# A written-out issue order for batches 2 to 30 of a cross-attention kernel, which gives VectorE's long subtraction another place beside GpSimd's operations

## The chip, the cores and the metric

The kernel runs on one core of a Trainium2 chip. The metric is the device time of one execution in microseconds (us). Five engines of the core take their instructions each from a queue of its own and in order: TensorE (matrix products; PE in the profile, its weight loads PEld), VectorE (DVE), ScalarE (ACT), GpSimd (POOL) and SyncE (SP), which here only issues DMAs. An instruction that waits on a semaphore holds back everything behind it in its queue.

## The reference

For each of 32 batches there are 512 query rows of x with 640 columns, and 77 context rows with 1024 columns. Queries come from x, keys and values from the context; 20 heads of 32 columns; softmax over the 77 keys; the heads' outputs go through an output matrix, and bias and x are added. The reference also names three more groups of keys, which are empty here because there are only 77 context rows. All data are float32.

```
q = heads(x @ to_q_w); k = heads(ctx @ to_k_w); v = heads(ctx @ to_v_w)
p = softmax(q k^T / sqrt(32))
out = merge(p v) @ to_out_w + to_out_b + x
```

## The kernel before

**Precision.** Every float32 matrix product is done as three products of a high and a low part. The high part is a rounded copy (ScalarE), the low part is the rest, value minus high part (VectorE or GpSimd).

**Stages.** A first stage of about 250 us projects the context into keys and values, which go to scratch in DRAM. Then come 160 slots, n = 0 to 159: five slots j = 0 to 4 for each batch b, n = 5b + j. Slot n does heads 4j to 4j+3 of its batch, and because the work is a pipeline, it does parts of several slots at once:

- queries of slot n+1: 15 matmuls (L443, `queries`), their split in `split_q`: high part on ScalarE (L454), two copies on GpSimd (L458), two low parts on VectorE (L460);
- scores of slot n, four tiles of 128 queries (L478, `scores`), each followed by a row maximum on VectorE (L486) and by four exponentials on ScalarE (L496, `exps`);
- softmax of slot n-1: reciprocal of the sums on VectorE (L506, `sums`), normalisation on GpSimd (L511, `normalize`), transposition on VectorE (L518, `transpose_p`), four stores to DRAM (L525);
- the probabilities of slot n-3 are loaded back from DRAM (L534 and L535, `load_p`), for use one slot later;
- those of slot n-4 are split: high parts on ScalarE (L542 and L543, `cast_p`), the small low part on GpSimd (L556, `last_p`), the large low part on VectorE (L549, `rest_p`, 128 x 1024: this is the long low-part subtraction). Then come six matmuls with the values (L570, `values`), and their two halves are added (L581 on ScalarE, L583 twice on VectorE, `sum_a`);
- the attention output of slot n-5 is split (L590 on ScalarE, `high_a`; L595 on VectorE, `low_a`). L595 reads the same PSUM tile that the six value matmuls of slot n-4 then write, and there is one such tile, so these matmuls wait for L595;
- eight steps of three matmuls of the output projection of an earlier batch (L613, `project`, in the order of `STEPS`), closed by VectorE's addition of bias and residual (L642) and by a store.

For the next batch, x is loaded (L253), transposed on VectorE (L257) and split (L264 on ScalarE, L265 on GpSimd). GpSimd also adds the bias to the residual (L606) and copies halves of the keys (L423, L424).

**Order.** The tile framework's scheduling is off (`manual_schedule`): each engine runs its instructions in the order in which the program issues them, and the framework only places the semaphores. `slot(n)` writes this order, the same for every batch from the third on. On VectorE, for one slot, it is: maximum 0, reciprocal, maximum 1, the long subtraction (L549), L595, maximum 2, two query low parts, maximum 3, transposition, then two halves of `sum_a` (in slots j = 4, L595 stands ahead of maximum 1). On GpSimd it is: last_p, normalize, two query copies, then bias or x work. Since `rs = sums(n - 1)`, `last_p` and `normalize` stand together in the program, and `rest_p` behind the second score tile:

```
s = scores(n, 0)
...
rs = sums(n - 1) if n else None
...
    last_p(taken)
...
    normalize(n - 1, rs)
exps(n, 0, *s)
...
s = scores(n, 1)
if taken is not None:
    rest_p(taken)
```

Of the kernel before, what the change touches and what calls it, by code (L numbers as in the profile page):

```python
# [8 lines left out]
F32 = mybir.dt.float32  # L9
FPR = mybir.dt.float32r  # L10
AF = mybir.ActivationFunctionType
ALU = mybir.AluOpType
# [39 lines left out]
def kernel(  # L52
# [202 lines left out]
    def transpose_x(b, i):  # L255
        part = xss[b][:, 4 * i : 4 * i + 4, :].rearrange("p a u -> p (a u)")
        nc.vector.transpose(part, part)  # L257

    def split_x(b, c, high=nc.scalar.copy, low=nc.gpsimd):

        xt = xpool[0].tile([P, 2, S], FPR, tag="xt", name="xt", bufs=7)
        src = xss[b].rearrange("p (a t) u -> p t a u", t=NQ)[:, :, :, c * Q : (c + 1) * Q]
        parts = [xt[:, i, :].rearrange("p (t a j) -> p t a j", t=NQ, j=Q) for i in range(2)]
        high(parts[0], src)  # L264
        low.tensor_tensor(parts[1], src, parts[0].bitcast(F32), ALU.subtract)  # L265
        xts[b, c] = xt

    ctx.enter_context(tc.manual_schedule(engines=ENGINES))

# [120 lines left out]
    psv = tc.alloc_tile_pool(name="psv", bufs=3, space=PSUM, side="right", reuse_waits="tile")  # L390
    late = []

    raws, pps, ats, pds, sms, pqs, pas, xrs, pos = ({} for _ in range(9))

    bias = main.tile([P, C], F32, name="bias")
    kbs, vbs, pnb = [], [], []
# [11 lines left out]
        vb = main.tile([P, nj, 2, 2, P], FPR, name=f"vb{g}")  # L408
        vbs.append(vb)

    def load_keys(b, g, heads=range(HPC)):
        j0, nj = GROUPS[g]
        src = k_dram[g][:, :, :, b * NKEY : (b + 1) * NKEY].bitcast(F32)
        kb = kbs[g].bitcast(F32)
        for i in heads:
            own, half = slice(i * HD, (i + 1) * HD), slice(i % 2 * NKEY, (i % 2 + 1) * NKEY)
            other = slice(*((i + 2) % HPC * HD + k for k in (0, HD)))
            for part, rows in enumerate((own, other)):
                nc.sync.dma_start(kb[rows, 1 + i // 2, :, half], src[own, part])

    def copy_keys(g):
        kb = kbs[g]
        nc.gpsimd.tensor_copy(kb[:64, 0], kb[:64, 1].bitcast(F32))  # L423
        nc.gpsimd.tensor_copy(kb[64:, 3], kb[64:, 2].bitcast(F32))  # L424

    def load_values(b, g, segments=SEGMENTS):
        j0, nj = GROUPS[g]
# [9 lines left out]
    def queries(n, k0, k1):  # L437
        b, j = divmod(n, NC_)
        if k0 == 0:
            pqs[n] = ps.tile([P, S], F32, tag="pq", name="pq", bufs=1)  # L440
        for k in range(k0, k1):
            for m, (a, c) in enumerate(PAIRS):
                nc.tensor.matmul(  # L443
                    pqs[n],
                    wq_s[:, k, a, j * P : (j + 1) * P],
                    xts[b, k][:, c, :],
                    start=(k == 0 and m == 0),
                    stop=(k == NC_ - 1 and m == 2),
                )
# [11 lines left out]
                qt[r, 1 + w, :], pq[r], qt[r, 0, :].bitcast(F32), ALU.subtract  # L461
            )

    def scores(n, t):
        b, j = divmod(n, NC_)
        g = GROUP_OF[j]
        qt, kb = qts[n % 2], kbs[g]
        jg = j - GROUPS[g][0]
        sc = ps.tile([P, S], F32, tag="sc", name="sc", bufs=3)
        half = KCOLS // 2  # L470
        for m, (cols, keys_) in enumerate(
            (
                (slice(0, KCOLS), kb[:, 0::3, jg]),
                (slice(0, half), kb[:, 1, jg]),
                (slice(half, KCOLS), kb[:, 2, jg]),
            )
        ):
            nc.tensor.matmul(  # L478
                sc[:, cols],
                qt[:, m, t * P : (t + 1) * P],  # L480
                keys_,
                start=(m == 0),
                stop=(m == 2),
            )
        nm = main.tile([P, HPC], F32, tag="nm", name="nm", bufs=3)
        nc.vector.tensor_reduce(  # L486
            nm, sc[:, :KCOLS].rearrange("p (h k) -> p h k", k=NKEY), AX.X, ALU.max, negate=True
        )
        return sc, nm

    def exps(n, t, sc, nm):
        if t == 0:
            sms[n] = main.tile([P, NQ * HPC], F32, tag="sm", name="sm", bufs=2)
        for i in range(HPC):
            at = t * HPC + i
            nc.scalar.activation(  # L496
                pnb[n % 2][:, at, :NKEY],
                sc[:, i * NKEY : (i + 1) * NKEY],
                AF.Exp,
                bias=nm[:, i : i + 1],  # L500
                accum_out=sms[n][:, at : at + 1],
            )

    def sums(n):
        rs = main.tile([P, NQ * HPC], F32, tag="rs", name="rs", bufs=2)
        nc.vector.reciprocal(rs, sms.pop(n))  # L506
        return rs

    def normalize(n, rs):
        pf = pnb[n % 2][:, :, :NKEY]  # L510
        nc.gpsimd.tensor_tensor(  # L511
            pf, pf, rs.unsqueeze(2).to_broadcast([P, NQ * HPC, NKEY]), ALU.mult
        )

    def transpose_p(n):
# [6 lines left out]
        pd = dram.tile([(NBLK + 2) * Q, S], F32, tag="pd", name="pd", bufs=6)  # L522
        rows = pd[: NBLK * Q].rearrange("(b i) q -> i b q", i=Q)
        for a in range(4):
            nc.sync.dma_start(  # L525
                rows[:, :, a * P : (a + 1) * P],
                z[a * Q : (a + 1) * Q].rearrange("p b t j -> p b (t j)"),
            )
        pds[n] = pd

    def load_p(n):
        pd = pds.pop(n)
        raw = late[0].tile([P, 3, S], F32, tag="raw", name="raw", bufs=2)
        nc.sync.dma_start(raw[:, 0:2, :], pd.rearrange("(k p) q -> p k q", k=2)[:P])  # L534
        nc.sync.dma_start(raw[:64, 2, :], pd[P : P + 64, :])  # L535
        raws[n] = raw

    def cast_p(n):

        raw = raws[n]  # L540
        pp = late[0].tile([P, 5, S], FPR, tag="pp", name="pp", bufs=1)
        nc.scalar.copy(pp[:64, 4, :], raw[:64, 2, :])  # L542
        nc.scalar.copy(pp[:, 0:2, :], raw[:, 0:2, :])  # L543
        pps[n] = pp

    def rest_p(n):

        raw, pp = raws.pop(n), pps[n]
        nc.vector.tensor_tensor(  # L549
            pp[:, 2:4, :], raw[:, 0:2, :], pp[:, 0:2, :].bitcast(F32), ALU.subtract  # L550
        )

    def last_p(n):

        raw, pp = raws[n], pps[n]
        nc.gpsimd.tensor_tensor(  # L556
            pp[64:, 4, :], raw[:64, 2, :], pp[:64, 4, :].bitcast(F32), ALU.subtract
        )
# [2 lines left out]

    PASSES = [(p, t, c + p * (t == 0)) for t, c in ((0, 0), (1, 4), (0, 2)) for p in range(2)]

    def values(n):
        b, j = divmod(n, NC_)
        g = GROUP_OF[j]
        pp, vb = pps.pop(n), vbs[g][:, j - GROUPS[g][0]]
        pas[n] = late[1].tile([P, 2, S], F32, tag="pa", name="pa", bufs=1)
        for p, t, c in PASSES:
            nc.tensor.matmul(  # L570
                pas[n][:, p, :],
                vb[:, p, t, :],
                pp[:, c, :],
                start=(c == p),
                stop=(c == p + 2),
            )

    def sum_a(n):
        pa = pas[n]
        aw = late[0].tile([64, 2, S], F32, tag="aw", name="aw", bufs=1)  # L580
        nc.scalar.copy(aw, pa[64:])  # L581
        for p in range(2):
            nc.vector.tensor_tensor(pa[64 * p : 64 * p + 64, 0], pa[:64, p], aw[:, p], ALU.add)  # L583

    def high_a(n):
        if n >= N - NC_ + 1:
            at = xpool[0].tile([P, 2, S], FPR, tag="xt", name="at", bufs=7)
        else:
            at = late[0].tile([P, 2, S], FPR, tag="at", name="at", bufs=8)
        nc.scalar.copy(at[:, 0, :], pas[n][:, 0])  # L590
        ats[n] = at

    def low_a(n):
        at = ats[n]
        nc.vector.tensor_tensor(  # L595
            at[:, 1, :], pas.pop(n)[:, 0], at[:, 0, :].bitcast(F32), ALU.subtract
        )

    def load_residual(b, t, xr=None):
# [28 lines left out]
    def piece(b, i):  # L628
        for t, h, j in STEPS[CUTS[i] : CUTS[i + 1]]:
# [3 lines left out]
            if j == NC_ - 1:  # L633
                closed.append((b, t, h))

    def finish():

        while closed:
            b, t, h = closed.pop(0)
            xr = xrs[b, t]  # L640
            cols = slice(h * HALF, (h + 1) * HALF)
            nc.vector.tensor_tensor(  # L642
                xr[:, cols], pos.pop((b, t, h))[:, :HALF], xr[:, cols], ALU.add
            )
            if (b, t) == (B - 1, NQ - 1):
                nc.sync.dma_start(out[b, t * P : (t + 1) * P, cols], xr[:, cols])
            elif h == 1:
                nc.sync.dma_start(out[b, t * P : (t + 1) * P, :], xr)

    LATE = 3  # L650
    LAG = 4
# [36 lines left out]
    def slot(n, beside=()):  # L688
# [135 lines left out]
        for i in turns[2]:  # L824
            transpose_x(b + 1, i)

    def end():


# [146 lines left out]
```

## Time and profile before

| | |
|---|---|
| three runs | 1928.79, 1928.88 and 1929.89 us, median 1928.88 us |
| profiled execution | span of 1928.2 us from its first to its last instruction; its time outside the span is not listed apart |
| TensorE matmul | 1882.9 us busy |
| VectorE, ScalarE, GpSimd | 1619.6, 1527.4 and 1423.9 us busy |
| HBM | 222 GB/s over the span |

The span is one execution; the runs are others, and their median lies 0.7 us above that span. Busy times are sums over stages that differ: the first 250 us have little softmax in them, and the last slots drain the pipeline. Between 354.3 and 1770.2 us the program repeats the same batch 28 times; the tables of the prediction are taken from there.

### The profile page before, as it was taken

What the parts mean: (1) busy time and instruction counts of PE and PEld (TensorE: products, weight loads), DVE (VectorE), ACT (ScalarE), POOL (GpSimd) and SP (SyncE); (2) the same over time, 40 slices, a digit from 0 to 9 for tenths busy, and PEclk for the clock granted to TensorE, in tenths of its full rate; (3) what the DMA queues carried; (4) which work ended last, traced back from release to release, by engine and by line L of the source; (5) the groups of instructions that cost most, each with busy time, mean ns of one, the idle gap of its engine ahead of it and who ended that gap; (6) DMA issues with size and microseconds to landing.
All of it is one profiled execution on the core that took longest, in us unless ns stands there. A gap on an engine that the chain in (4) does not pass through costs nothing.

```text
span 1928.2 us, 37543 instructions
## 1 busy us (share of the span) xinstructions
PE 1882.9 (98%) x10332; PEld 1663.1 (86%) x10332; DVE 1619.6 (84%) x2494; ACT 1527.4 (79%) x6210; POOL 1423.9 (74%) x1116
## 2 busy tenths in 40 slices
PE   9999997999999999999999999999999999999997
PEld 7888896898888888888888888988888888888887
DVE  4444447899999999999999999999999899999885
ACT  3232248998889898898898889998999889989883
POOL 1100067888888888888888888888888888888874
PEclk9999998999999999999999999999999999999999
DMA  9978868989999899888998998988889989988875
GB/s 185 205 194 248 198 180 218 229 232 234 233 225 235 231 232 225 229 234 231 233 231 228 228 238 236 237 231 232 237 232 227 228 223 232 227 231 229 225 202 166
DMA packets 565022, 431.36 MB, mean 224 GB/s; under 512 B 191120, under 2 KB 473168, under 8 KB 564816
## 3 DMA queue, kind: packets, MB, share of 16 engines
q1 hardware_dynamic: 559760, 413.62, 84.9%
q0 software_dynamic: 4416, 14.34, 2.2%
q8 instruction: 85, 1.39, 0.3%
q14 instruction: 121, 0.99, 0.2%
q10 hardware_dynamic: 640, 1.02, 0.2%
HBM read 247.17 MB, written 181.64 MB: 222 GB/s over the span
## 4 chain that ended last, share of the span: by engine, by line
PE 38%; DMA 22%; ACT 14%; DVE 9%; SPq 7%; POOL 5%; issue 5%; ACTq 0%; DVEq 0%; POOLq 0%
PE po L613 10%; PE pq L443 9%; DMA raw<-pd 8%; DMA xs<-in_x_dram 7%; ACT pn L496 6%; PE pv L191 5%; PE pk L191 5%; PE pa L570 4%; PE sc L478 4%; DVE pp L549 3%; DMA kb<-k_dram 2%; ACT pp L543 2%; SPq L432 2%; ACT pp L542 1%; ACT xt L264 1%
## 5 line engine op out<-in xcount | busy, mean ns | idle before, releaser
L496 ACT ACTIVATE pn<-sc,nm 128x77 f32<-128x77 f32 x2560 | 793.8, 332 | 46.6 <-DVE nm L486 40.6
L613 PE MATMUL po<-wo_s,at 128*128 128x320 f32 x3840 | 635.1, 314 | 12.1 <-DVE at L595 9.0
L443 PE MATMUL pq<-xt,wq_s 128*128 128x512 f32 x2400 | 623.7, 401 | 0.0
L613 PEld LDWEIGHTS po<-wo_s,at 128*128 128x128 f32 x3840 | 568.3, 189 | 20.4 <-DVE at L595 17.4
L496 ACT ACTIVATION_READ_ACCUMULATOR pn<-sc,nm 128x1 f32 x2560 | 544.6, 213 | 0.0
L511 POOL TENSOR_TENSOR pn<-pn,rs 128x1232 f32<-128x1232 f32 x160 | 507.7, 3173 | 33.3 <-DVE rs L506 24.2
L443 PEld LDWEIGHTS pq<-xt,wq_s 128*128 128x128 f32 x2400 | 431.3, 190 | 76.1
L478 PEld LDWEIGHTS sc<-kb,qt 128*128 128x128 f32 x1920 | 327.8, 189 | 57.2 <-POOL qt L458 8.7
L478 PE MATMUL sc<-kb,qt 128*128 128x154 f32 (+1 forms) x1920 | 318.1, 274 | 11.0 <-POOL qt L458 4.5
L486 DVE TENSOR_REDUCE nm<-sc 128x4 f32<-128x308 f32 x640 | 287.7, 450 | 37.7 <-PE sc L478 33.2
L549 DVE TENSOR_TENSOR pp<-raw,pp 128x1024 fp32r<-128x1024 f32 x160 | 253.1, 1582 | 40.7 <-ACT pp L543 38.7
L556 POOL TENSOR_TENSOR pp<-raw,pp 64x512 fp32r<-64x512 f32 x160 | 209.3, 1308 | 100.2 <-ACT pp L542 90.5
L570 PE MATMUL pa<-pp,vb 128*128 128x512 f32 x960 | 263.7, 404 | 15.3 <-DVE at L595 10.1
L518 DVE STREAM_TRANSPOSE z<-pn 128x1280 f32<-128x1280 f32 x160 | 241.8, 1511 | 9.3 <-DMA pd<-z 2.7
L460 DVE TENSOR_TENSOR qt<-pq,qt 64x512 fp32r<-64x512 f32 x320 | 219.1, 685 | 29.0 <-ACT qt L454 22.7
L583 DVE TENSOR_TENSOR pa<-pa,aw 64x512 f32<-64x512 f32 x320 | 222.6, 696 | 24.3 <-ACT aw L581 14.0
L265 POOL TENSOR_TENSOR xt<-xs,xt 128x512 fp32r<-128x512 f32 x160 | 202.6, 1291 | 37.1 <-ACT xt L264 32.5
L570 PEld LDWEIGHTS pa<-pp,vb 128*128 128x128 f32 x960 | 169.7, 188 | 63.4 <-DVE pp L549 15.4
L606 POOL TENSOR_TENSOR xr<-xr,bias 128x640 f32<-128x640 f32 x128 | 202.7, 1585 | 17.3 <-DMA xr<-in_x_dram 5.4
L458 POOL CAST qt<-qt 64x512 fp32r<-64x512 f32 x320 | 194.8, 609 | 23.7 <-ACT qt L454 4.2
L581 ACT COPY aw<-pa 64x1024 f32<-64x1024 f32 x160 | 161.9, 1012 | 48.2 <-PE pa L570 44.1
L542 ACT CAST pp<-raw 64x512 fp32r<-64x512 f32 x160 | 99.5, 622 | 99.7 <-DMA raw<-pd 95.6
(46 smaller groups left out, 1640.9 us busy)
## 6 DMA issues: line engine op xcount, KB each, us to landing
pd<-z SPq DMA_DIRECT2D x640, 160.0 KB, 3.5
raw<-pd SPq DMA_DIRECT2D x160, 512.0 KB, 4.3
xs<-in_x_dram SPq DMA_DIRECT2D x128, 320.0 KB, 7.4
xr<-in_x_dram SPq DMA_DIRECT2D x128, 320.0 KB, 3.7
out_dram<-xr SPq DMA_DIRECT2D x127, 320.0 KB, 3.7
raw<-pd SPq DMA_DIRECT2D x160, 128.0 KB, 4.3
v_dram<-vs SPq DMA_DIRECT2D x80, 192.0 KB, 4.0
k_dram<-ks POOLq DMA_DIRECT2D x20, 512.0 KB, 4.2
```

What stands on the lines that cost most here:

```text
L443: nc.tensor.matmul(pqs[n], wq_s[:, k, a, j * P : (j + 1) * P], xts[b, k][:, c, :], start=(k == 0 and m == 0), stop=(k == NC_ - 1 and m == 2),)
L460: nc.vector.tensor_tensor(qt[r, 1 + w, :], pq[r], qt[r, 0, :].bitcast(F32), ALU.subtract)
L478: nc.tensor.matmul(sc[:, cols], qt[:, m, t * P : (t + 1) * P], keys_, start=(m == 0), stop=(m == 2),)
L486: nc.vector.tensor_reduce(nm, sc[:, :KCOLS].rearrange("p (h k) -> p h k", k=NKEY), AX.X, ALU.max, negate=True)
L496: nc.scalar.activation(pnb[n % 2][:, at, :NKEY], sc[:, i * NKEY : (i + 1) * NKEY], AF.Exp, bias=nm[:, i : i + 1], accum_out=sms[n][:, at : ...
L511: nc.gpsimd.tensor_tensor(pf, pf, rs.unsqueeze(2).to_broadcast([P, NQ * HPC, NKEY]), ALU.mult)
L518: nc.vector.transpose(z.rearrange("p b t j -> p t b j"), pn.rearrange("p (t h) k -> p t (h k)", t=NQ).rearrange("p t (b i) -> p t b i", i=Q),)
L549: nc.vector.tensor_tensor(pp[:, 2:4, :], raw[:, 0:2, :], pp[:, 0:2, :].bitcast(F32), ALU.subtract)
L556: nc.gpsimd.tensor_tensor(pp[64:, 4, :], raw[:64, 2, :], pp[:64, 4, :].bitcast(F32), ALU.subtract)
L570: nc.tensor.matmul(pas[n][:, p, :], vb[:, p, t, :], pp[:, c, :], start=(c == p), stop=(c == p + 2),)
L583: nc.vector.tensor_tensor(pa[64 * p : 64 * p + 64, 0], pa[:64, p], aw[:, p], ALU.add)
L613: nc.tensor.matmul(pos[b, t, h][:, :HALF], ats[b * NC_ + j][:, a, t * P : (t + 1) * P], wos[0][:, j, c, h * HALF : (h + 1) * HALF], start= ...
```

## The change

The functions are cut into smaller ones that issue one step each (`score_tile` and `score_max`, `block_transpose` and `store_p`, `load_rows`, `cast_rows`, `value_pass`, `lower_half` and `add_halves`, `high_x` and `low_x`, and so on). For slots 0 to 9 and 155 to 159 `slot` still calls them in the old order. For batches 2 to 30 a table `PLAN` gives the order of all 344 steps of a batch, the same for each of the 29 batches, and `issue` carries one step out. The steps, their instructions and their sizes are those of before, and their number in a batch is the same; only the order in each queue differs.

A token is the slot j, a letter and numbers. On TensorE: q queries (a chunk of 3 matmuls), s score tile (3), v value matmul (1), p projection step (3). On VectorE: m maximum, r reciprocal, **R the long subtraction (L549)**, L low_a (L595), z transposition, g query low part, a half of sum_a, f addition to the output, T transposition of x. On ScalarE: e exponentials of a tile, c0 and c1 casts (L542, L543), A lower half (L581), h high_a, Q query high part, X high part of x. On GpSimd: **N normalisation (L511), l small low part (L556)**, k query copy, b bias, x low part of x, K key copy. On SP: w and d store and load of the probabilities, o store of the output, ux, ur, uk and uv loads of x, residual, keys and values.

```diff
+    PLAN = (
+        "0p16 0c0 0q0 0c1 0s0 0p17 0m0 0h 0l 0d0 0s1 0e0 0q1 0m1 0uk131 0r 0q2 0f10 0uk121 0N 0R "
+        "1uv11 0q3 0uk130 0q4 0ur3 0L 0ux3 0s2 0Q 0d1 0s3 0m2 0e1 0p18 0g0 0v1 0v0 0k1 0v2 0g1 1uv12 "
+        "0p20 0e2 0k0 0v3 0z 0v4 0v5 0b2 0p19 0A 1s0 1q0 0w1 0m3 1c1 0a0 0w0 0p21 1uv13 1s1 0f11 0e3 "
+        "0p22 1R 0w2 1q1 0uk110 1c0 0w3 0p23 1r 1m0 1N 1d0 1q2 1m1 1e0 1uv17 0a1 1q3 0uk101 0T0 1p25 "
+        "1h 0uk100 1q4 1e1 1T1 1uv14 1l 1s2 1d1 1L 1p26 0o1 1Q 1s3 1m2 1uv16 1p27 1k1 1e2 1m3 1p24 "
+        "1g0 1k0 2d0 1v1 1v3 1g1 0uk120 1v0 1e3 1b3 1v2 1p28 1uv15 1z 1v4 2s0 1v5 2q0 1A 2r 1w0 1f20 "
+        "2q1 2N 2d1 2m0 2c0 1T2 1p29 1w1 2e0 2q2 2uv07 1a1 2s1 1uv10 2c1 2q3 1a0 1w2 2l 1ur0 2s2 2T3 "
+        "2h 2q4 1w3 2m1 1K11 2uv06 1p30 2f21 2Q 1K10 1p31 2uv03 2L 2X0 2p32 2k0 2o2 2m2 2X1 2p33 "
+        "0uk111 2R 2k1 2p35 2uv04 2e1 2p36 2uv02 2g0 2v1 2v0 3d0 2e2 2v3 2x1 2g1 2v2 2p37 2v4 2z 2v5 "
+        "2p38 2b0 2A 2p39 2s3 3c0 3q0 3uk031 2m3 2x0 2a1 3q1 3uk010 3X2 2w0 3s0 3c1 3ur1 3l 2p34 3s1 "
+        "2w1 2e3 2f30 3q2 2w2 3m0 2a0 2w3 3q3 3e0 3d1 3r 3p0 3f31 3N 3R 3q4 3uk001 3h 3uk020 3s2 3X3 "
+        "3L 3o3 3p4 2uv01 3Q 3p5 3m1 3p1 3m2 3e1 3p2 3g0 2uv05 3v1 3uk021 3s3 3g1 3k0 3uk011 3e2 3v0 "
+        "3v2 4d0 3m3 3v4 3x2 3v3 2uv00 3v5 3z 3X4 4q0 3uk000 3A 3p6 3k1 4q1 3w0 3x3 4c0 3a1 3w2 4s0 "
+        "3e3 4q2 3w1 3a0 3x4 3p7 3uk030 4m0 4h 4s1 4ur2 4q3 4c1 4m1 3w3 4l 4L 4ux0 4s2 4e0 4q4 4r 4m2 "
+        "4ux1 4R 4N 3p3 4Q 4p8 4d1 4e1 4v0 4ux2 4f00 4p9 4v1 4g1 4s3 4e2 4v2 4f01 4v3 4v4 4g0 4p10 "
+        "4k0 4m3 4v5 4p11 4A 4z 4K00 4p12 4p13 4K01 4e3 4p15 4k1 4w2 4p14 4a0 4w3 4b1 4a1 4o0 4w0 4w1 "
+    ).split()
...
+    def issue(b, token):
+        j, op, arg = int(token[0]), token[1], [int(c) for c in token[2:] if c.isdigit()]
...
+        elif op == "R":
+            rest_p(old)
+        elif op == "v":
+            value_pass(old, arg[0])
...
-    for n in range(LATE, N):
+    for n in range(LATE, 2 * NC_):
+        slot(n)
+    for b in range(2, B - 1):
+        while closed:
+            closed.pop()
+        for token in PLAN:
+            issue(b, token)
+    closed.extend(OPEN)
+    for n in range(N - NC_, N):
         slot(n)
     end()
```

On VectorE the table places R behind r and an output addition in slots 0 and 3 (`0r 0f10 0R`, `3r 3f31 3R`), ahead of r in slot 1 (`1R 1r 1m0`), late in slot 2 (`2L 2m2 2R`), and behind r and the third maximum in slot 4 (`4L 4r 4m2 4R`). On GpSimd, l stands ahead of N in slots 0, 3 and 4 and behind it in slots 1 and 2.

More of the change, by code (lines that the diff above doesn't have):

```diff
@@ L521, in transpose_p, with store_p, load_rows, cast_rows @@
         )
[L522 to L544 removed]
+    def store_p(n, a):
+        if n not in pds:
+            pds[n] = dram.tile([(NBLK + 2) * Q, S], F32, tag="pd", name="pd", bufs=6)
+        rows = pds[n][: NBLK * Q].rearrange("(b i) q -> i b q", i=Q)
+        nc.sync.dma_start(
+            rows[:, :, a * P : (a + 1) * P],
+            z[a * Q : (a + 1) * Q].rearrange("p b t j -> p b (t j)"),
+        )
+    def transpose_p(n):
+        block_transpose(n)
+        for a in range(4):
+            store_p(n, a)
+    def load_rows(n, part):
+        if n not in raws:
+            raws[n] = late[0].tile([P, 3, S], F32, tag="raw", name="raw", bufs=2)
+        raw, pd = raws[n], pds[n]
+        if part == 0:
+            nc.sync.dma_start(raw[:, 0:2, :], pd.rearrange("(k p) q -> p k q", k=2)[:P])
+        else:
+            nc.sync.dma_start(raw[:64, 2, :], pd[P : P + 64, :])
+    def load_p(n):
+        load_rows(n, 0)
+        load_rows(n, 1)
+    def cast_rows(n, part):
+        if n not in pps:
+            pps[n] = late[0].tile([P, 5, S], FPR, tag="pp", name="pp", bufs=1)
+        raw, pp = raws[n], pps[n]
+        if part == 0:
+            nc.scalar.copy(pp[:64, 4, :], raw[:64, 2, :])
+        else:
+            nc.scalar.copy(pp[:, 0:2, :], raw[:, 0:2, :])
+    def cast_p(n):
+        cast_rows(n, 0)
+        cast_rows(n, 1)
     def rest_p(n):
[L548 removed]
+        raw, pp = raws[n], pps[n]
         nc.vector.tensor_tensor(
@@ L562, with value_pass, values, lower_half @@
     PASSES = [(p, t, c + p * (t == 0)) for t, c in ((0, 0), (1, 4), (0, 2)) for p in range(2)]
-    def values(n):
+    def value_pass(n, i):
         b, j = divmod(n, NC_)
         g = GROUP_OF[j]
[L567 to L576, printed above, removed]
-    def sum_a(n):
[L579 to L583, printed above, removed]
+        pp, vb = pps[n], vbs[g][:, j - GROUPS[g][0]]
+        if n not in pas:
+            pas[n] = late[1].tile([P, 2, S], F32, tag="pa", name="pa", bufs=1)
+        p, t, c = PASSES[i]
+        nc.tensor.matmul(
+            pas[n][:, p, :],
+            vb[:, p, t, :],
+            pp[:, c, :],
+            start=(c == p),
+            stop=(c == p + 2),
+        )
+    def values(n):
+        for i in range(len(PASSES)):
+            value_pass(n, i)
+    def lower_half(n):
+        aws[n] = late[0].tile([64, 2, S], F32, tag="aw", name="aw", bufs=1)
+        nc.scalar.copy(aws[n], pas[n][64:])
+    def add_halves(n, p):
+        pa, aw = pas[n], aws[n]
+        nc.vector.tensor_tensor(pa[64 * p : 64 * p + 64, 0], pa[:64, p], aw[:, p], ALU.add)
+    def sum_a(n):
+        lower_half(n)
+        add_halves(n, 0)
+        add_halves(n, 1)
     def high_a(n):
```

144 lines of the change are left out of this document (120 added, 24 removed).

## The prediction

> **What bounds the kernel now.** I read the busy times first, then the waits of one engine, then the pace of its instructions. TensorE leads:
>
> ```profile
> PE 1882.9 (98%) x10332; PEld 1663.1 (86%) x10332; DVE 1619.6 (84%) x2494; ACT 1527.4 (79%) x6210; POOL 1423.9 (74%) x1116
> ```
>
> 98% does not say that nothing can be had, because matmuls overlap. The table of stretches (28 batches together, then one quick batch; stretch, its length, busy times, clock, DMA share, GB/s) and the waits of TensorE's weight loads in the same two stretches (total, times, longest) tell more:
>
> ```profile
> 354.30:1770.20 1415.90, 1399.22 (x7982) 1248.63 (x7981) 1309.22 (x2017) 1269.52 (x5320) 1212.49 (x925) 1.00 0.90 231
> 1162.80:1212.40 49.60, 49.46 (x287) 44.52 (x286) 46.83 (x73) 45.77 (x191) 43.63 (x34) 1.00 0.89 234
> ```
>
> ```profile
> PEld po L613 <- DVE at L595: 14.4, 24, 1.4
> PEld pa L570 <- DVE pp L549: 13.6, 27, 0.6
> PEld pa L570 <- DVE at L595: 9.8, 20, 1.8
> PEld pa L570 <- POOL pp L556: 2.1, 4, 0.8
> ```
>
> ```profile
> PEld pa L570 <- DVE pp L549: 0.6, 1, 0.6
> ```
>
> The first four rows are the 28 batches: 14.4 + 13.6 + 9.8 + 2.1 = 39.9 us, 1.43 us a batch, nearly all for VectorE: the long subtraction R (L549) and L (L595). A batch takes 1415.9 / 28 = 50.57 us. Less its waits that is 49.14; the quick batch gives 49.6 - 0.6 = 49.0. So a microsecond of these waits is a microsecond of time, and about 49.1 is what the matmuls take. Their own pace (start, length) says the same:
>
> ```profile
> 1002.10 2.28 PE L443 MATMUL pq<-xt,wq_s 128*128 128x512 f32 x9
> 1004.22 0.49 PE L478 MATMUL sc<-kb,qt 128*128 128x308 f32 x3
> 1004.54 2.05 PE L613 MATMUL po<-wo_s,at 128*128 128x320 f32 x12
> 1006.44 1.56 PE L570 MATMUL pa<-pp,vb 128*128 128x512 f32 x6
> 1007.84 0.48 PE L478 MATMUL sc<-kb,qt 128*128 128x308 f32 x3
> 1008.15 1.96 PE L613 MATMUL po<-wo_s,at 128*128 128x320 f32 x12
> 1009.95 0.49 PE L478 MATMUL sc<-kb,qt 128*128 128x308 f32 x3
> ```
>
> From start to start: 2.12 us for nine query matmuls, 0.706 a token q; 0.31 to 0.32 a token s; 1.40 for six value matmuls, 0.233 a token v; 1.80 for the later twelve of the projection, 0.45 a token p. A batch has 25 q, 20 s, 30 v and 40 p: 17.65 + 6.4 + 7.0 + 18.0 = 49.05 us.
>
> **Why R is late.** Three places of the timeline (start, length):
>
> ```profile
> 963.99 1.29 POOL L556 TENSOR_TENSOR pp<-raw,pp 64x512 fp32r<-64x512 f32 x1
> 964.24 2.13 DVE L549 TENSOR_TENSOR pp<-raw,pp 128x1024 fp32r<-128x1024 f32 x1 [0.38 <-ACT pp L543]
> 965.36 3.14 POOL L511 TENSOR_TENSOR pn<-pn,rs 128x1232 f32<-128x1232 f32 x1
> ...
> 972.67 0.23 DVE L506 RECIPROCAL rs<-sm 128x16 f32<-128x16 f32 x1
> 972.84 0.41 DVE L486 TENSOR_REDUCE nm<-sc 128x4 f32<-128x308 f32 x1
> 973.08 3.43 POOL L511 TENSOR_TENSOR pn<-pn,rs 128x1232 f32<-128x1232 f32 x1
> 973.17 1.20 DVE L549 TENSOR_TENSOR pp<-raw,pp 128x1024 fp32r<-128x1024 f32 x1
> ...
> 983.43 1.73 POOL L424 CAST kb<-kb 64x308 fp32r<-64x308 f32 x1 [3.01 <-DMA kb<-k_dram]
> 983.65 1.20 DVE L549 TENSOR_TENSOR pp<-raw,pp 128x1024 fp32r<-128x1024 f32 x1
> ```
>
> The same N (L511) over all 28 batches, shortest, median and longest in ns:
>
> ```profile
> L511 POOL TENSOR_TENSOR pn<-pn,rs x140: 2272/3139/3465, 360.6 to 1764.7; 128x1232 f32<-128x1232 f32 x140
> ```
>
> First place: R starts 0.25 us into l (L556) and takes 2.13; it ends at 966.37, 1.09 us after l's end (965.28). Read: it stood until l was done, then ran. N, which opened meanwhile, took 3.14 where it can take 2.27. Second place: R starts 0.09 us after N, takes 1.20, and N ends 2.14 us after R's end: here N stood. Third: R starts 0.22 us after a key copy and goes first too. So the two engines take turns, and an operation of GpSimd has an opening, 0.1 to 0.2 us after its start, in which R still goes first.
>
> **The change part by part.** No instruction is added or taken away. What moves is the order on five queues. I laid the PE tokens of the table end to end by the paces above (0 is 0p16; the batch ends at 49.0) and put the other queues beside them with the lengths of these rows (mean ns behind the bar). A score tile is read 0.5 us after its token starts (the 0.49 of its rows), and a DVE operation starts up to 0.08 before the one ahead of it ends (973.17 against 972.84 + 0.41).
>
> ```profile
> L486 DVE TENSOR_REDUCE nm<-sc 128x4 f32<-128x308 f32 x560 | 251.5, 449 | 29.3 <-PE sc L478 25.3
> ...
> L583 DVE TENSOR_TENSOR pa<-pa,aw 64x512 f32<-64x512 f32 x280 | 194.8, 696 | 9.2
> ...
> L642 DVE TENSOR_TENSOR xr<-po,xr 128x320 f32<-128x320 f32 x224 | 102.4, 467 | 0.0
> L595 DVE TENSOR_TENSOR at<-pa,at 128x512 fp32r<-128x512 f32 x140 | 95.1, 680 | 5.7 <-ACT at L590 5.5
> L257 DVE STREAM_TRANSPOSE xs<-xs 128x640 f32<-128x640 f32 x112 | 92.6, 827 | 0.0
> ```
>
> ```profile
> L543 ACT CAST pp<-raw 128x1024 fp32r<-128x1024 f32 x140 | 147.0, 1050 | 0.0
> L581 ACT COPY aw<-pa 64x1024 f32<-64x1024 f32 x140 | 141.7, 1012 | 25.3 <-PE pa L570 21.5 <-PE sc L478 1.1
> ```
>
> - Slot 0. 0s1 starts at 1.93, so m1 runs from 2.43 to 2.88 and r starts at 2.80. By the second place N starts 0.41 after r starts, at 3.21. R comes behind an addition (0.47, where the maximum there took 0.41): 0.50 + 0.06 = 0.56 after r starts, at 3.36, which is 0.15 after N. If it goes first, it ends at 4.56 and L (0.68) at 5.2. The first matmul that needs L is 0v1 at 6.16: 1.0 us to spare. N ends at 4.56 + 2.14 = 6.7.
> - Slot 3. 2f30 waits for 2p34 (30.71 + 0.45): it starts near 31.3; then m0 and a0, and r starts at 31.3 + 0.47 + 0.45 + 0.70 - 0.24 = 32.7; N 33.1, R 33.25 to 34.45, L to 35.1; 3v1 is at 36.16: 1.0 to spare.
> - Slot 4. 4s1 is at 41.22, m1 runs from 41.7 to 42.2, L to 42.8; 4p8, the projection step that takes L, is at 43.72: 0.9 to spare. This was the wait of 14.4 us, and R now stands behind L. R follows r and m2 (4s2 at 42.25): 43.1 to 44.3; 4v4 reads it at 45.87.
> - Slot 1. R runs ahead of r, so ahead of N. It has its cast at 0v5 (7.77) + 0.4 + 1.01 (A) + 1.05 (c1) = 10.2. Behind it come r, m0, m1, a, two T and L: 0.23 + 0.90 + 0.70 + 1.65 + 0.68 less 0.5 of overlaps, 3.7. Then L ends at 10.2 + 1.2 + 3.7 = 15.1; 1v1 is at 16.42.
> - Slot 2. L stands ahead of R and ends near 24; 2v1 is at 25.91. R meets two query copies of GpSimd and can lose the length of one to them.
>
> So all waits on R and L go, with about 0.9 us of room. What is late next: the query copies k1 and k0 (some 0.6 each) behind N in slot 0, 6.7 to 7.9, for 1s0 at 8.46. If N is over 0.6 later still, TensorE waits for GpSimd.
>
> *ScalarE.* The exponentials of tile 1 stand behind Q, which waits for q4, so ScalarE idles 1.5 to 2 us in slots 0 and 4. Its free time (79% busy) and the third score buffer hide that; if they are gone, a third score tile waits, up to those 2 us.
>
> *DMAs.* SP's queue is rearranged throughout, and each issue passes others (median us from issue to landing at the end of a row):
>
> ```profile
> raw<-pd SPq DMA_DIRECT2D x160, 512.0 KB, 4.3
> xs<-in_x_dram SPq DMA_DIRECT2D x128, 320.0 KB, 7.4
> ```
>
> Most loads have 5 us or more. The tightest: 4d1, issued near 44.0 behind two loads of x, for 0c0 at 49.2 (5.2 us, against 4.3, or 7.4 if it lands with x: 2.2 late). Then c0 and c1 end 2.2 later, R starts 0.7 later, and slot 0 keeps 0.3 of its room. 0ux3, issued near 5, must land before the first T at 13. The DMA engines are busy 0.90 of the time at 231 GB/s in the 28 batches and 0.89 at 234 in the quick one: no bound at 49.4 us.
>
> *Matmul switches.* A batch has 74 changes from one kind of matmul to another, before 45, in pairs that no row has. The nearest: the same three score matmuls take 0.31 or 0.32 before different kinds. I take nothing, and 0.02 each way as the ends: 29 x 0.02 = 0.6 us a batch, 17 us.
>
> *Sum.* 29 batches x 1.43 = 41.5 us if all goes. Loads that land late bring some waits back: I keep half of what the quick batch has, 0.3. Then 29 x 1.1 = 32 us: the span goes from 1928.2 to 1896, and the median, 0.7 above the span, to 1897. Ends: 1928.9 - 41.5 = 1887, and with the switches 1914.
>
> **The rivals.**
>
> 1. *R loses in slots 0 and 3* (slower). The trace shows R first at 0.09 us after N; the table gives 0.15; the only place beyond (0.22) is a copy, and against l R lost at 0.25. If it loses, it stands until N ends: 3.21 + 2.27 = 5.48, R to 6.57, L to 7.2 against 0v1 at 6.16: 1.0 us. Slot 3: N to 35.4, R to 36.5, L to 37.1 against 36.16: 1.0. With the 0.3 that stays, waits are 2.3 a batch: 29 x 0.9 = 26 us slower, 1955. It decides from the point where R starts after N's opening. If one slot of the two loses: 1.3 a batch, 1926. The Trainium skill puts it more sharply (SBUF — State Buffer, "Who interferes with whom": whoever issues first gets the shared port pair for the whole instruction, the other fully blocks): by that rule, read with the start times shown, this rival would be the forecast. The second and third places disagree with that reading, since there the later starter went first, by 0.09 and 0.22 us.
> 2. *Late loads eat the room* (three quarters of the gain): 4d1, or the stores ahead of the next z, cost 0.35 a batch more: 1907.
> 3. *The table does not do what it says*: R still meets N's opening in slots 0, 3 and 4, and N stands 1.2 us there. For: the sums above say that it does. Against its cost: among the waits, TensorE stood for GpSimd 2.1 us in 28 batches. GpSimd then has the 0.6 us of room that the forecast counts with.
>
> **How the numbers follow.** Forecast 1897 (1887 to 1905): 0.64. Rival 2 and the switches (1905 to 1915): 0.11. One slot lost (1926): 0.07. Rival 1 (1955): 0.13. Something slower that I do not see: 0.05. The range 1886 to 1932 holds the first three, 0.82. A measurement of this kernel can tell about 0.2%, 4 us. Faster than that: 0.64 + 0.11 = 0.75; within: 0.07; slower: 0.18.
>
> **What would show it.** Right: R near 1.2 us in four slots of five, the waits on L595 and L549 almost gone from the weight loads' list, N at 3.3 to 3.5 us in slots 0 and 3, batches of 49.3 to 49.5 us. Wrong: R at 3 us beside N at 2.27 (rival 1); ScalarE's casts waiting for raw, or z for the stores (rival 2); score tiles waiting for the query copies (GpSimd is the bound); batches above 49.5 us without waits (the switches cost).

## The result, and the profile after

The changed kernel takes **1999.82 us** (median of 4 runs, 1997.87 to 2000.97) where the kernel before takes 1928.84 (4 runs beside it, 1926.46 to 1929.89): ratio **1.0374, 95% interval 1.0359 to 1.0389**. It is 71 us slower; 32 us faster had been forecast.

In the profile after, lines have new numbers: the long subtraction R is L589 (before L549), L is L646 (L595), N is L535 (L511), the reciprocal r L530 (L506), the value matmuls L611 (L570). Busy times of the profiled execution (span 1996.1 us, time 1997.87):

```profile
PE 1894.0 (95%) x10332; PEld 1660.0 (83%) x10332; DVE 1718.0 (86%) x2494; ACT 1538.4 (77%) x6210; POOL 1385.5 (69%) x1116
```

TensorE is busy for 11 us more, so most of the time is new waiting, and VectorE has gained 98 us of busy time with the same 2494 instructions: they don't do more, some of them last longer. Table of stretches, first 19 equal batches, then one quick batch, and what the weight loads waited for in the first stretch (total, times, longest):

```profile
665.60:1676.70 1011.10, 959.13 (x5415) 844.78 (x5415) 959.70 (x1369) 868.58 (x3612) 795.87 (x628) 1.00 0.86 220
1728.20:1779.20 51.00, 49.98 (x287) 44.65 (x286) 46.79 (x73) 45.25 (x190) 44.76 (x36) 1.00 0.90 232
```

```profile
PEld pa L611 <- DVE at L646: 43.7, 38, 1.2
PEld pa L611 <- DVE pp L589: 23.8, 19, 1.3
PEld pq L460 <- ACT pn L520: 10.3, 19, 0.5
PEld po L664 <- DVE xr L689: 4.1, 19, 0.2
```

A batch takes 1011.1 / 19 = 53.22 us (before 50.57). The four waits add up to 81.9 us, 4.31 a batch, and 53.22 - 4.31 = 48.91, close to the 49.0 to 49.14 of before: the loss is waiting. The counts say where: every batch stands twice for L, once for R, once for an exponential, once for an output addition. Which instruction started this is seen in the lengths of R and N (shortest, median, longest in ns):

```profile
L589 DVE TENSOR_TENSOR pp<-raw,pp x130: 1195/3226/3280, 365.6 to 1733.8; 128x1024 fp32r<-128x1024 f32 x130
```

```profile
L535 POOL TENSOR_TENSOR pn<-pn,rs x131: 2273/2277/3474, 358.2 to 1734.1; 128x1232 f32<-128x1232 f32 x131
```

"R at 3 us beside N at 2.27" is what the prediction gave as the sign of its first rival. It holds in slots 0 and 3, and in slot 4 too. The three places in the timeline (start, length), first VectorE, then GpSimd; slot 0, slot 3, slot 4:

```profile
1000.36 0.24 DVE L530 RECIPROCAL rs<-sm 128x16 f32<-128x16 f32 x1
1000.52 0.43 DVE L689 TENSOR_TENSOR xr<-po,xr 128x320 f32<-128x320 f32 x1
1000.86 3.23 DVE L589 TENSOR_TENSOR pp<-raw,pp 128x1024 fp32r<-128x1024 f32 x1
...
1032.14 3.23 DVE L589 TENSOR_TENSOR pp<-raw,pp 128x1024 fp32r<-128x1024 f32 x1
1035.29 0.68 DVE L646 TENSOR_TENSOR at<-pa,at 128x512 fp32r<-128x512 f32 x1
...
1043.99 3.28 DVE L589 TENSOR_TENSOR pp<-raw,pp 128x1024 fp32r<-128x1024 f32 x1
```

```profile
1000.74 2.27 POOL L535 TENSOR_TENSOR pn<-pn,rs 128x1232 f32<-128x1232 f32 x1 [0.77 <-DVE rs L530]
...
1032.01 2.28 POOL L535 TENSOR_TENSOR pn<-pn,rs 128x1232 f32<-128x1232 f32 x1 [1.31 <-DVE rs L530]
...
1043.91 2.28 POOL L535 TENSOR_TENSOR pn<-pn,rs 128x1232 f32<-128x1232 f32 x1 [1.48 <-ACT pp L580]
```

R starts 0.12, 0.13 and 0.08 us behind N, stands until N is done and then runs: in slot 3, 1032.01 + 2.28 = 1034.29, and R ends 1.08 later at 1035.37. What the weight loads pay for slots 3 and 4:

```profile
1036.02 0.19 PEld L611 LDWEIGHTS pa<-pp,vb 128*128 128x128 f32 x1 [1.19 <-DVE at L646]
1038.16 0.53 PEld L460 LDWEIGHTS pq<-xt,wq_s 128*128 128x128 f32 x3 [0.53 <-ACT pn L520]
1047.32 0.19 PEld L611 LDWEIGHTS pa<-pp,vb 128*128 128x128 f32 x1 [1.26 <-DVE pp L589]
1047.72 0.44 PEld L664 LDWEIGHTS po<-wo_s,at 128*128 128x128 f32 x3 [0.21 <-DVE xr L689]
```

In the stretch of 1728.2 to 1779.2 R happened to go first in slots 4 and 0, and that batch took 51.0 us. Over the 29 batches of the table R goes second in 27 places each of slots 0, 3 and 4.

### The profile page after: what moved, and what is told of

It reads as the page before. It is cut to its first block, busy times and chain, and to the rows that moved or that the text cites. A ratio compares the mean times of both kernels' runs of the same rounds, so it can differ in the third digit from the quotient of the medians.

```text
span 1996.1 us, 37193 instructions
## 1 busy us (share of the span) xinstructions
PE 1894.0 (95%) x10332; PEld 1660.0 (83%) x10332; DVE 1718.0 (86%) x2494; ACT 1538.4 (77%) x6210; POOL 1385.5 (69%) x1116
## 4 chain that ended last, share of the span: by engine, by line
PE 61%; DVE 20%; ACT 8%; DMA 4%; issue 3%; SPq 2%; POOL 1%; DVEq 0%; ACTq 0%; POOLq 0%
PE po L664 19%; PE pq L460 15%; DVE pp L589 10%; PE pa L611 9%; PE pk L191 7%; PE pv L191 6%; PE sc L495 6%; ACT pn L520 4%; DMA pd<-z 3%; DVE nm L506 2%; DVE at L646 2%; DVE xr L689 2%; SPq L550 1%; DVE z L541 1%; DVE pa L629 1%
## 5 line engine op out<-in xcount | busy, mean ns | idle before, releaser
L664 PE MATMUL po<-wo_s,at 128*128 128x320 f32 x3840 | 692.9, 312 | 3.1 <-ACT at L641 1.9
L460 PE MATMUL pq<-xt,wq_s 128*128 128x512 f32 x2400 | 661.3, 400 | 3.8
L664 PEld LDWEIGHTS po<-wo_s,at 128*128 128x128 f32 x3840 | 605.8, 189 | 49.0 <-DVE xr L689 5.8
L520 ACT ACTIVATION_READ_ACCUMULATOR pn<-sc,nm 128x1 f32 x2560 | 567.1, 222 | 0.0
L535 POOL TENSOR_TENSOR pn<-pn,rs 128x1232 f32<-128x1232 f32 x160 | 378.0, 2363 | 227.3 <-DVE rs L530 184.6
L611 PE MATMUL pa<-pp,vb 128*128 128x512 f32 x960 | 308.8, 413 | 76.4 <-DVE at L646 51.5
L589 DVE TENSOR_TENSOR pp<-raw,pp 128x1024 fp32r<-128x1024 f32 x160 | 363.7, 2273 | 3.1 <-ACT pp L580 2.9
L506 DVE TENSOR_REDUCE nm<-sc 128x4 f32<-128x308 f32 x640 | 284.3, 458 | 21.7 <-PE sc L495 18.1
L951 POOL CAST qt<-qt 64x512 fp32r<-64x512 f32 x290 | 268.7, 927 | 39.6 <-ACT qt L948 25.2
L611 PEld LDWEIGHTS pa<-pp,vb 128*128 128x128 f32 x960 | 170.2, 190 | 120.1 <-DVE at L646 63.2
L954 DVE TENSOR_TENSOR qt<-pq,qt 64x512 fp32r<-64x512 f32 x290 | 198.2, 683 | 4.5 <-ACT qt L948 0.9
L580 ACT CAST pp<-raw 128x1024 fp32r<-128x1024 f32 x160 | 168.9, 1056 | 0.1
```

The costliest lines, as they stand in the source:

```text
L460: nc.tensor.matmul(pqs[n], wq_s[:, k, a, j * P : (j + 1) * P], xts[b, k][:, c, :], start=(k == 0 and m == 0), stop=(k == NC_ - 1 and m == 2),)
L506: nc.vector.tensor_reduce(nm, sc[:, :KCOLS].rearrange("p (h k) -> p h k", k=NKEY), AX.X, ALU.max, negate=True)
L520: nc.scalar.activation(pnb[n % 2][:, at, :NKEY], sc[:, i * NKEY : (i + 1) * NKEY], AF.Exp, bias=nm[:, i : i + 1], accum_out=sms[n][:, at : ...
L535: nc.gpsimd.tensor_tensor(pf, pf, rs.unsqueeze(2).to_broadcast([P, NQ * HPC, NKEY]), ALU.mult)
L589: nc.vector.tensor_tensor(pp[:, 2:4, :], raw[:, 0:2, :], pp[:, 0:2, :].bitcast(F32), ALU.subtract)
L611: nc.tensor.matmul(pas[n][:, p, :], vb[:, p, t, :], pp[:, c, :], start=(c == p), stop=(c == p + 2),)
```

## The experiments

**Theories.** A: the whole loss is R standing behind N in slots 0, 3 and 4. B: the rest of the new order (DMAs, switches of TensorE, the table) costs part of it. If A holds, a second question: what decides who goes first when R starts 0.03 to 0.13 us behind N, since the kernel before has R first at 0.11 to 0.12 in slots 0 and 2? Times are compared with the kernel before on the same chip, since chips differ: it ran at 1918.7 us beside e1 to e4, and between 1929.2 and 1933.2 beside the later ones. e1 and e3 were run 4 and 10 times, all others once.

**e1: R first.** In slots 0, 3 and 4 R stands directly behind r; additions go ahead of r, slot 4's maximum behind R.

```diff
-0m1 0uk131 0r 0q2 0f10 0uk121 0N 0R
+0m1 0uk131 0f10 0r 0R 0q2 0uk121 0N
-3r 3p0 3f31 3N 3R
+3f31 3r 3R 3p0 3N
-4r 4m2 4ux1 4R 4N
+4r 4R 4m2 4ux1 4N
```

> The table with R (the long subtraction) directly behind the reciprocal r in slots 0, 3 and 4, so that it starts about 0.2 us ahead of N (the normalisation on GpSimd) instead of 0.08 to 0.13 us behind it; the additions that stood between r and R in slots 0 and 3 go ahead of r, the maximum of slot 4 behind R. Theory A (the loss is R standing behind N in these three slots): R takes 1.2 us in all five slots, the waits of the weight loads on VectorE fall under 0.5 us a batch, a batch takes 49.3 to 49.6 us (53.2 less 1.5 for slot 3 and 2.4 for slots 4 and 0, which single batches of the changed kernel show where R went first), and the time is 1888 to 1905 us. Theory B (the new order costs by its other parts: finer switches of matmuls, loads issued later, ScalarE idle behind Q): R is short and the time stays above 1960 us.

Measured: 1895.17 us against 1918.66, ratio 0.9873 (0.9856 to 0.9889): 1.3% less than the kernel before, and far below the 2000 us of the changed one. R's lengths, a stretch of 21 batches (1036.2 / 21 = 49.34 us), and the one wait of weight loads in it:

```profile
L589 DVE TENSOR_TENSOR pp<-raw,pp x140: 1152/1206/1530, 367.0 to 1739.2; 128x1024 fp32r<-128x1024 f32 x140
```

```profile
697.60:1733.80 1036.20, 1035.81 (x5987) 936.98 (x5986) 952.70 (x1513) 955.92 (x3992) 888.61 (x694) 1.00 0.90 237
```

```profile
PEld sc L495 <- POOL qt L951: 1.7, 5, 0.6
```

PE is busy 1035.81 of 1036.20 us. A holds: the queues of TensorE and of the DMAs have the same order as in the changed kernel, and nothing is left to wait for but the score tile behind the query copies, 0.08 us a batch. B can at most have a small part: without its waits a batch takes 49.34 - 0.08 = 49.26 us, 0.1 to 0.3 more than the 49.0 to 49.14 of before. Whether the switches or something else take that is not shown.

**e3: the old order through the table**, all 344 tokens in the order of before.

> The old order of a batch, written as a table and issued step by step for batches 2 to 30. Theory A and B alike: the table is only an order, so the time is that of before, 1926 to 1932 us. If issuing in small steps costs by itself (more semaphores, other waits), it is above 1935 us, and part of the loss lies there.

Measured: 1916.3 us, ratio 0.9982 (0.9972 to 0.9991). The table itself costs nothing. The waits of its weight loads from 354.3 to 1700 us, 27 batches, tell something else:

```profile
PEld pa L611 <- DVE pp L589: 13.0, 27, 0.8
PEld pa L611 <- DVE at L646: 8.2, 20, 1.8
PEld po L664 <- DVE at L646: 7.4, 19, 1.2
```

On this chip the old order waits 28.6 us for R and L, 1.06 us a batch, where the profile before had 13.6 + 9.8 + 14.4 = 37.8 in 28, 1.35 a batch. There was less to be had here: 29 x 1.06 = 31 us. e1 has none of these waits left and is 21 us faster than e3, 23.5 us faster than the kernel before; most of the rest fits its longer batch without waits (29 x 0.2 = 6 us).

**e5 and e6: one place alone.** e5 takes e1's edit in slot 3 only, e6 in slot 0 only.

> In slot 3 alone R (the long subtraction) stands directly behind the reciprocal r, ahead of the normalisation N's start, and the addition f31 ahead of r; slots 0 and 4 stay as in the changed kernel. The changed kernel's batch is 53.2 us, and R lost against N in slots 0, 3 and 4. If the three losses are independent of each other, slots 0 and 4 lose again (R at 3.2 us there), and the batch loses only slot 3's 1.5 us: 51.7 us, some 43 us below the changed kernel, about 1950. If they are a chain, in which slot 3's delay moves what comes after it, R goes first in slots 4 and 0 too: batches near 49.3 us and a time of 1890 to 1905, as with all three places mended. In the changed kernel's own trace the two batches after a slot 3 that R had won went this way.

> The counterpart: R directly behind r in slot 0 alone; slots 3 and 4 as in the changed kernel. The addition ahead of R stays in slot 3, so by the theory that the kind of operation ahead of R decides, R loses there (3.2 us), and the batch gets shorter by slot 0's share alone, 1.0 to 1.5 us: 51.7 to 52.2 us, a time of 1950 to 1970. If slot 0 were the head of the chain: R first in slots 3 and 4 too, batches near 49.3 us and 1890 to 1905.

Measured: e5 1901.6 and e6 1974.25 us (4 above the range expected), the kernel before 1933.16. In e5 R goes first in all 29 places of slot 4 (1215 to 1257 ns) and in 20 of 29 of slot 0; in e6 it goes on losing in 25 of 29 places of slot 3 and 25 of 29 of slot 4. In the changed kernel and in e6, slots 3 and 4 of a batch are always lost or won together. So the loss of slot 4 hangs on slot 3's, and that of slot 0 in most batches: once R has gone first there, l runs until shortly before N in slot 4, N is late, and R starts 0.21 to 0.25 us ahead of it. What is left in e5 from 360 to 1740 us is slot 0's share, 1.1 us each time:

```profile
PEld pa L611 <- DVE at L646: 8.9, 8, 1.1
```

**What decides the race?** e2 leaves 32 of 320 columns out of the two additions ahead of R, which brings R nearer to N; e4 puts a maximum in the addition's place in slots 0 and 3.

```diff
 e4
-3r 3p0 3f31 3N 3R
+3f31 3r 3p0 3m1 3N 3R
```

> The table as it is, but the output addition ahead of R in slots 0 and 3 leaves out 32 of its 320 columns (of batches 0 to 28, output columns 288 to 319 of row block 1 and 608 to 639 of row block 3 miss the attention part), so that it ends about 33 ns earlier: some 0.17 us after N's start instead of 0.20. Theory A1 (who is first is decided within some 10 ns: in all rows so far R goes first where the operation ahead of it ends up to 0.194 us after N starts, and stands where it ends from 0.200 us on): R goes first in slots 0 and 3 and takes 1.2 us; 1890 to 1945 us, by whether slot 4 follows. Theory A2 (the kind of the operation ahead decides: behind an addition R loses, behind a maximum it wins): R still takes 3.2 us in slots 0 and 3, time 1995 to 2002 us.

> The table with a maximum between r and R in slots 0 and 3, as in the order of before, and the addition ahead of r. Slot 4 stays. The maximum ends some 0.19 us after N starts. Theories A1 and A2 both: R goes first in slots 0 and 3 and takes 1.2 us there; 1890 to 1945 us by whether slot 4 follows. If it still takes 3.2 us, what is ahead of R is not what decides, and something about N (its waits, its data) does.

Measured: e2 2002.72 us, R lost in 54 of 55 near races of slots 0 and 3, 0.083 to 0.095 us behind N. e4 1894.41 us; R first in slot 3 in all 28 near races, at 0.112 to 0.117 us, and slots 0 and 4 followed. This looked like proof that the kind of operation ahead of R decides, and it was not: e10 puts a short addition ahead of R in slots 0 and 2 of the old order, and e11 puts the maximum between r and R in slot 3 without moving the addition ahead of r.

```diff
 e10 (old order; f10 and f21 leave out 32 of 320 columns)
-0m1 0R ... 0f10   and   2f21 2o2 2r ... 2m1 2R
+0f10 0R 0m1       and   2r ... 2f21 2o2 2R 2m1
 e11
-3r 3p0 3f31 3N 3R
+3r 3p0 3m1 3N 3R 3f31
```

> The old order, issued through the table (with the maximum ahead of R it took 0.9982 of the kernel before, and R went first in slots 0 and 2 at 0.11 to 0.12 us behind N's start), with one change in those two slots: an addition stands ahead of R in the maximum's place, and the maximum behind R. The addition leaves out 32 of its 320 columns, so that R starts no later than it did, some 0.09 us behind N. If the kind of the operation ahead decides in the kernel, R now loses there (3.2 us in place of 1.2) wherever it starts 0.03 to 0.12 us behind N. If the distance or the place in the table decides, R goes on going first.

> The changed kernel with one edit in slot 3: a maximum stands between r and R, the addition f31 behind R; ahead of r stands the addition of halves a, as in the changed kernel. In all traces so far R won its near races (R 0.03 to 0.13 us behind N) where r had started 65 to 76 ns before the end of the operation ahead of it (162 of 165), and lost where it had started 82 to 86 ns before that end (nearly all of 172); behind a it always does the latter. If the operation between r and R decides, R goes first here in slot 3, slots 0 and 4 follow, and the time is 1890 to 1905. If what stands ahead of r decides, R loses in slot 3 as in the changed kernel, and the time stays near 2000.

Measured: e10 1931.43 us (before 1929.46), R first behind an addition in all 34 near races. e11 2054.37 us (before 1932.85), R lost behind the maximum in all 28 near races of slot 3, at 0.111 to 0.117 us; it costs more than the changed kernel because f31 now stands behind the losing R and the projection waits for it. The same five operations of e4, where R went first, and of e11, where it lost (VectorE, then GpSimd):

```profile
1039.80 0.47 DVE L689 TENSOR_TENSOR xr<-po,xr 128x320 f32<-128x320 f32 x1
1040.20 0.23 DVE L530 RECIPROCAL rs<-sm 128x16 f32<-128x16 f32 x1
1040.36 0.41 DVE L506 TENSOR_REDUCE nm<-sc 128x4 f32<-128x308 f32 x1
1040.69 1.20 DVE L589 TENSOR_TENSOR pp<-raw,pp 128x1024 fp32r<-128x1024 f32 x1
```

```profile
1040.58 3.46 POOL L535 TENSOR_TENSOR pn<-pn,rs 128x1232 f32<-128x1232 f32 x1 [0.61 <-DVE rs L530]
```

```profile
1002.36 0.69 DVE L629 TENSOR_TENSOR pa<-pa,aw 64x512 f32<-64x512 f32 x1
1002.97 0.23 DVE L530 RECIPROCAL rs<-sm 128x16 f32<-128x16 f32 x1
1003.13 0.41 DVE L506 TENSOR_REDUCE nm<-sc 128x4 f32<-128x308 f32 x1
1003.46 3.23 DVE L589 TENSOR_TENSOR pp<-raw,pp 128x1024 fp32r<-128x1024 f32 x1
```

```profile
1003.35 2.27 POOL L535 TENSOR_TENSOR pn<-pn,rs 128x1232 f32<-128x1232 f32 x1 [1.03 <-DVE rs L530]
```

From r to R the two are the same within 0.01 us, and so is N's start behind r (0.38). The visible difference is what stands ahead of r: an addition, which r overlaps by 0.07 us, or a, which it overlaps by 0.08.

**The race alone.** e7, e8, e9 and e13 leave out the kernel and repeat r, one operation of growing width, N and R, with what each text adds; e7 went wrong by its own design, as the text of e8 says.

> Leaves out the whole computation (the output is zeros) and measures the disputed cost by itself: N and R alone, behind a reciprocal and one operation of VectorE that reads the PSUM: a maximum, an addition with a second input in SBUF, or a copy with SBUF output alone, each from 96 to 496 columns, so that R starts at growing distances behind N's start. If the distance alone decides, R goes from 1.2 us to 3.2 us at the same distance for the three kinds. If the kind decides (R behind an addition loses, behind a maximum wins), the distance at which it turns differs: for the maximum over 0.12 us, for the addition below 0.09 us, and the copy, with one input, tells whether it is the input or the output in SBUF that counts. If there is no such difference, the cause lies in what stood elsewhere in the kernel, and stays open.

> Leaves out the whole computation (the output is zeros). The measurement of the opening again, mended: in the first one a loss delayed the cast that R waits for, so that every later R came 0.87 us behind N's start, and only its first sixteen rounds say something. Here R waits for no cast, and each round begins with all engines done with the round before. Twelve kinds of round: the operation between the reciprocal r and R is a maximum, a two-input addition or a copy (32 to 496 columns); r comes after an idle VectorE or directly behind another maximum; N waits for r alone or for an earlier operation of GpSimd as well, which gives it a wait instruction of its own, as in the kernel. If the distance from N's start alone decides, all twelve turn from R at 1.1 us to R at 3.2 us at one distance. If the kind ahead decides, the additions turn below 0.09 us and the maxima above 0.12 us. If it is the form of N's wait, the two forms turn at different distances with any kind ahead (the first measurement, with the single wait, turned between 0.017 and 0.034 us). If an idle VectorE ahead of r decides (slot 4, where r stands directly behind a maximum, lost with a maximum ahead of R at 0.08 us), the two kinds of r differ.

> Leaves out the whole computation (the output is zeros). Alone, N and R turned at one distance, 0.02 to 0.03 us after N's start, whatever the kind ahead, the form of N's wait and the idleness before r; in the kernel R still went first at 0.11 to 0.12 us behind a maximum and lost at 0.08 to 0.13 us elsewhere. So something around them lengthens the opening in some places of the kernel. The rounds are repeated in five stages: quiet, with stores of 2 x 256 KB a round, with four exponentials of ScalarE a round, with nine matmuls a round (the maximum then reads what a matmul has just written, and waits for TensorE), and with all three. If the DMAs slow the start of N, the turn moves to 0.1 us or more in the stages dma and all; if ScalarE does, in act and all; if a matmul's write or the wait on TensorE holds the maximum's place, in pe and all and for the maximum alone. If it stays at 0.02 to 0.03 us in all five, none of the three is the cause and it stays open.

Measured, by start times in the trace: e7's first sixteen rounds turn between 0.017 and 0.034 us. In e8 R goes first up to 0.022 us behind N and loses from 0.025 us on, in all twelve kinds of round; in e9 up to 0.022 and from 0.021 on, in all five stages. Two rounds of e8, an addition of 224 columns with R first (0.02 us behind N) and a maximum of 240 columns with R last (0.03 us); first VectorE, then GpSimd:

```profile
652.52 1.21 DVE L134 TENSOR_TENSOR low_add<-raw,high 128x1024 fp32r<-128x1024 f32 x1
...
700.45 3.31 DVE L134 TENSOR_TENSOR low_max<-raw,high 128x1024 fp32r<-128x1024 f32 x1
```

```profile
652.50 3.35 POOL L131 TENSOR_TENSOR pn<-pn,rs 128x1232 f32<-128x1232 f32 x1 [0.68 <-DVE rs L122]
...
700.42 2.27 POOL L131 TENSOR_TENSOR pn<-pn,rs 128x1232 f32<-128x1232 f32 x1 [1.71 <-DVE rs L122]
```

So alone there is one distance, about 0.02 us, and neither the kind ahead, nor the form of N's wait, nor DMAs, ScalarE or TensorE beside it move it.

**What stands ahead of r.** e12 and e14 try to change it with an addition kept between r and R (e12 moves f30 directly ahead of r; e14 puts f31 ahead of r and f30 between); e13 puts 0 to 4 maxima ahead of r in the race alone.

> The counterpart in slot 3: the addition f30 is moved directly ahead of r, and the addition f31 stays between r and R. If the operation between r and R decides, R loses in slot 3 and the time stays near 2000. If what stands ahead of r decides (behind an addition of this kind r started 75 ns before its end in slot 3, and R went first), R goes first though it starts 0.125 us behind N: R 1.2 us in slot 3, slots 0 and 4 follow, 1890 to 1905.

> Leaves out the whole computation (the output is zeros). All near races of the kernels so far (R 0.025 to 0.2 us behind N) fall out by one number, how long VectorE had been running without a break when r started: up to 0.8 us, or one operation, R lost 361 of 364; at 0.99 to 1.01 us (two operations) it won 119 and lost 35; from 1.38 us on it won all 70. The two measurements alone had at most one operation ahead of r and turned at 0.02 us. Here 0, 1, 2, 3 or 4 maxima of 0.39 us stand ahead of r, with a maximum or an addition between r and R. If the unbroken run decides, the turn stays near 0.02 us for 0 and 1, and lies beyond 0.12 us for 3 and 4, with either kind between. If it stays at 0.02 us for all, the run is a mark of something else in the kernel.

> In the kernel, slot 3 alone: f31 moves ahead of r, and the addition f30 comes between r and R, so that a, f31, r, f30 and R follow each other without a break: VectorE runs for 1.0 us before r, against 0.6 in the changed kernel, with an addition still between r and R at 0.125 us behind N. If the unbroken run decides, R goes first in most batches of slot 3, slots 0 and 4 follow, and the time is 1890 to 1910. If the addition between r and R decided, R would lose and the time stay near 2000.

Measured: e12 1999.07 and e14 1999.58 us (before 1932.85 for both), R lost in 28 of 29 places of slot 3 in each. Both missed their aim: r waited for ScalarE's sums and, but for one place, started 0.1 to 0.35 us after the operation ahead had ended. In that one place (e12) r started 75 ns before the end of the addition ahead, and R, 0.127 us behind N, lost all the same. e13 turns between 0.014 and 0.022 us with any number of maxima ahead: an unbroken run of VectorE is not the cause.

What stays is a mark in the trace. Over the ten traces of whole kernels taken for this study and the two of before and after, R started 0.025 to 0.2 us behind N with one operation between r and R in 673 places. Where r had started 65 to 76 ns before the end of the operation ahead of it, R went first in 191 of 198; where it had started 80 to 86 ns before, or after an idle stretch, R lost in 472 of 475. In e8 and e13 only the second kind occurs (80 to 85 ns, or idle). The mark goes with the outcome, and no run shows that it causes it: none in the race alone has the first kind among its near races. What makes r overlap less, and why R then still goes first 0.1 us behind N, stays open.

## Why the prediction was wrong

- **The floor and the gain, if R goes first: right.** "About 49.1 is what the matmuls take" and "all waits on R and L go, with about 0.9 us of room": e1, where R does go first, has no such wait left and a batch of 49.34 us. On its chip there were 1.06 us of waits a batch (e3) in place of 1.43; with the 0.3 kept back, as in the forecast, that gives 29 x (1.06 - 0.3) = 22 us, and e1 is 21 us under e3 and 23.5 under the kernel before. The 0.3 was kept for late loads, and e1 shows none. That the amount is about right all the same is luck: what is missing lies in the batch without its waits, 49.26 us against 49.0 to 49.14.
- **DMAs and the table: right; the switches: open.** e3 puts the table itself at -0.2%. Dearer switches would lengthen the matmuls and not the waits; by the 49.26 they cost at most 0.3 us a batch, less than the 0.6 allowed, and no run separates them.
- **The failed step:** "an operation of GpSimd has an opening, 0.1 to 0.2 us after its start, in which R still goes first", and from it, in slots 0 and 3, "R comes behind an addition ..., which is 0.15 after N. If it goes first". R came 0.12 and 0.13 us behind N and lost in 27 of 29 batches in each. The opening was read off two places of before, one of them (0.22) beside a key copy and not beside N; alone it is 0.02 us wide. The whole trace of before would have said more: beside N, R went first in all 49 places 0.04 to 0.121 us behind it, and last in one place 0.63 us behind it (at 317 us); nothing lay between, so 0.15 was an extrapolation. The first rival had the mechanism at a chance of 0.13, which was too low, though before shows no loss as near as these. The Trainium skill has its rule (SBUF — State Buffer, "Who interferes with whom"): whoever issues first gets the shared pair for the whole instruction. e8 agrees with it to within 0.025 us; in the kernels R went first against it in 194 of the 673 near places, 191 of them of the kind described above.
- **Slot 4: missed.** "R follows r and m2: 43.1 to 44.3" took 1.2 us for granted beside an N that starts 0.08 us earlier. That is a third loss in nearly every batch.
- **The rival's price: half.** It was 2.3 us of waits a batch and 1955 us. R's delay came as worked out (N's 2.27 and 1.08 more), and L's waits are 1.15 each against 1.0. Missing were slot 4's wait for R (23.8 / 19 = 1.25 us a batch) and what follows a late VectorE, the exponential in slot 3 and the additions, (10.3 + 4.1) / 19 = 0.76 us. 2.3 + 1.25 + 0.76 = 4.3, as measured. 53.22 - 50.57 = 2.65 us over 29 batches would be 77; the first batches and the two late ones in which R won lose less, and 71 are measured.
- **Not counted: the losses hang together.** A loss in slot 3 takes slot 4 with it, and mostly slot 0 (e5). So "if one slot of the two loses: 1926" has no price that fits both: slot 0 alone costs 1.1 us a batch, and with slots 3 and 4 lost e6 takes 1974.

## What to carry to other kernels

When two engines block each other, as R and N do here, a start that is 0.1 us late in a timeline cannot be counted on to win, even where one saw it win elsewhere. So set the order by a margin: hang the long operation directly behind the one that releases its rival (e1: R starts at least 0.22 us ahead of N) and let the rival pay, if it has the room. And where a batch is a chain of slots, ask for each place that may lose what it shifts into the next one.

## What the runs showed of the hardware

R that goes second lasts until 1.08 us after N's end, and N that goes second ends 2.12 to 2.15 us after R's: neither shares. Alone, the later starter can still win at up to 0.02 us; whether this is a real opening or only as well as start times of two engines compare is not shown. A maximum or an addition of VectorE that reads PSUM doesn't keep N waiting: in e8 N takes 2.27 us beside both. Not expected: the race falls the same way at one place for dozens of batches, and at the same distance the other way at another place: R first in slot 3 of e4 at 0.112 to 0.117 us, R last in slot 3 of e11 at 0.111 to 0.117.
